# Sums over keys placed directly in front of the mix of values, and a mix that leaves PSUM undivided

## The chip, the cores and the metric

The kernel runs on one core of a Trainium2 chip. The metric is the device time of one launch in microseconds (us). The kernel before took 2891.65 us, the median of three runs (2891.22 to 2893.65).

The engines are called as the profile calls them: PE is TensorE (matmuls and transposes; PEld are its weight loads), DVE is VectorE, ACT is ScalarE, POOL is GpSimd, SP is SyncE, which here only issues DMAs.

## The reference, cut to what matters

Two graph layers run over 64 graphs ("batches") of 256 nodes with 512 features in f32. The first is attention with 8 heads of 64 under one adjacency mask, the second a graph attention with one score per node pair. Each adds its input and normalises:

```python
q, k, v = (x @ Wq + bq), (x @ Wk + bk), (x @ Wv + bv)          # split into 8 heads of 64
scores = einsum('bqhd,bkhd->bhqk', q, k) / sqrt(64) + (1 - adj) * -1e9
attn = softmax(scores, axis=-1)                                 # over the keys
x = layernorm(x + einsum('bhqk,bkhd->bqhd', attn, v) @ Wo + bo)
h = x @ W
e = leaky_relu(s1[:, :, None] + s2[:, None, :]) * adj           # s1, s2: h times the halves of a
x = layernorm(x + elu(softmax(e, axis=2) @ h + beta * h))
```

The change touches the line with `attn` and the one below it: the division of the softmax by its sums over the keys, and the mix of values.

## The kernel before

Every batch goes through twelve named stages. Their names are those of `ROUND` (L23):

- **x**: `tr_x` transposes the input tile (L496) into xT.
- **q, k, v**: projections by `project` (L382 and L386). Each is written as seven products of quarter matrices, with the sums of quarters on POOL (`token_sums`, L360: xS, oS, yS) and the results combined by ACT copies and DVE additions (L517, L520, L526). The products lie in three PSUM tiles, ps_chain, ps_cross and ps_pair.
- **scores**: `ps_sc` (L574), keys on partitions, two heads at a time on the two halves of the array's rows (64*128). DVE adds the mask (L581), ACT takes the exponential (L583), POOL adds the two key tiles of a head into `both` (L585).
- **sums**: `ps_den` (L597), the sums over the keys, by matmuls against columns of ones, on four groups of 32 columns (128*32). DVE takes the reciprocal (L601), ACT notes the range of both (L604). A DMA writes the 8 rows to DRAM (L607) and two more bring them back spread over the partitions as `inv_all` (L611), in the code `everywhere`.
- **mix**: `ps_pv` (L551), values times exponentials, two heads at a time on the two halves of the columns (128*64). DVE multiplies the PSUM result by `everywhere` into oT (L617).
- **o**: the output projection from oT and its POOL differences oS, added to x on DVE (L700), then the layer norm (L456 to L466).
- **logits**: the two scores of a node by DVE (L715), their transposes `tr_s` (L725), then the mask, the maximum and the exponential on DVE, POOL and ACT.
- **attention**: `tr_a` transposes the probabilities (L753), ACT copies them to attT (L757).
- **spread**: `ps_y` (L768), probabilities times x; **u**: the projection by W; then elu, the norm and the store of the result.

The order is not left to the hardware. Every piece of work is registered with `plan.op` (engine, an assumed duration, what it reads and writes, and for PE a `mode`: the shape in which the array is used). PE's order is fixed by a pair per piece, the number of its round and the place of its stage in `ROUND`. The pair comes from `turn`, which adds to the batch's number n a delay in rounds: with "sums": 0 and "mix": 1, the sums of batch n are in round n and its mix in round n + 1. The other engines get due times from PE's order, and `place` lists everything greedily against slots of buffers (8 PSUM banks, 9 SBUF tiles of the tag "full", 24 of "half", 5 of x). The last 70 pieces of PE are ordered freely (`OPEN`). A round of the kernel before reads on PE:

    tr_a, mix, scores, tr_x, ps_y, o, u, sums, v, tr_s, q, k

Each of the stages works on a batch of its own: while the scores are those of batch n, the mix and o are those of n - 1, and tr_a, spread and u those of n - 2. In order that the mix can be multiplied by `everywhere` on its way out of PSUM, the reciprocals of a batch have to be back from DRAM when its mix ends; the piece "mix" on PE therefore lists `everywhere` among its reads.

[...]

There is a second form of the attention for inputs whose sums leave a safe range (`attention_by_queries`); it doesn't run with these inputs.

Of the kernel before, what the change touches and what calls it, by code (L numbers as in the profile page):

```python
# [19 lines left out]
ALPHA = 0.2  # L20
NEG = -1000000000.0

ROUND = ("mix", "scores", "x", "spread", "o", "u", "sums", "v", "logits", "q", "k", "attention")  # L23
SAFE = 1e15


# [196 lines left out]
def gnn_two_layers(ctx: ExitStack, tc: tile.TileContext, x, adj, Wq, bq, Wk, bk, Wv, bv, Wo, bo, W, a, beta, out):  # L223
    nc = tc.nc
# [23 lines left out]
    plan = Plan(slots)  # L248
    stay = []
    A = slice(None)  # L250

    def sb(tag, shape, name):
        return Buf(sb_pool, tag, [P] + shape, name)

    def ps(shape, name):
        return Buf(ps_pool, "ps", [P] + shape, name)
# [11 lines left out]
    def blk(t):  # L268
        return slice(t * P, (t + 1) * P)
# [142 lines left out]
    def residual_bias():  # L412
        bo_sb = for_now(bo, 0, "bo")
        acc = ps([D], "ps_b")

        def pe():
            for c in range(C):
                nc.tensor.matmul(acc[A], bv_sb[:, c:c + 1].to_broadcast([P, P]), wo_sb[:, c, :], start=c == 0,
                                 stop=c == C - 1)

        plan.op("PE", 3440, pe, [wo_sb], [acc], claims=[res_sb])
        plan.op("DVE", 690, lambda: nc.vector.tensor_add(res_sb[A], acc[A], bo_sb[A]), [acc, bo_sb], [res_sb])  # L422
        return weight_sums(wo_sb, "so_sb", "POOL", [res_sb])
# [46 lines left out]
    def batch(b, at, general=False):  # L470

        X = sb("x", [NT, D], f"x_{b}")
        n = b or 0

        def turn(what):

            later = {"x": -1, "q": -1, "k": -1, "scores": 0, "v": 0, "sums": 0, "mix": 1, "o": 1, "logits": 1,
                     "attention": 1, "spread": 2, "u": 2}[what]
            plan.turn = (n + later, ROUND.index(what if b != 0 or what != "sums" else "logits"))

        plan.op("SP", 2800, lambda: nc.sync.dma_start(X[A], x[at].rearrange("o (t p) d -> p (o t) d", p=P)), [],
                [(X, (t, i)) for t in range(NT) for i in range(2)], first=b == 0)
# [6 lines left out]
        V = sb("full", [NT, D], f"v_{b}")  # L489
# [14 lines left out]
        if b == 0:  # L504
            plan.turn = (0, ROUND.index("spread"))
            left["o"] = residual_bias()
# [27 lines left out]
        def val():  # L534
            turn("v")
            project(lv, right, False, [V], *gather(lambda q: (lambda: V[:, q[1], half(q[0])], (V, q))))


        oT = sb("full", [C, N], f"oT_{b}")

        def mixed(pT, g, onto, reads=()):

            turn("mix")
            acc = ps([2, N], "ps_pv")

            def pe():
                for i in range(2):
                    for k in range(NT):
                        for s in range(2):
                            h = 4 * g + 2 * i + s  # L550
                            nc.tensor.matmul(acc[s * HD:(s + 1) * HD, i, :], V[:, k, h * HD:(h + 1) * HD],  # L551
                                             pT[h][:, k, :], start=k == 0, stop=k == NT - 1)

            plan.op("PE", 1740, pe, [(V, (g, 0)), (V, (g, 1))] + pT[4 * g:4 * g + 4] + list(reads), [acc],
                    mode="columns", claims=[oT])
            plan.op("DVE", 690, lambda: onto(acc), [acc] + list(reads), [(oT, g)])

        def attention_by_keys():

            pT = [sb("half", [NT, N], "pT") for h in range(H)]  # L560
            both = [sb("half", [2, N], "both") for c in range(C)]
            inv, everywhere = sb("half", [N], "inv"), sb("full", [C, N], "inv_all")
            rows = Buf(dram_pool, "rows", [H, N], "rows")

            def scores(g):
                turn("scores")
                acc = [ps([NT, N], "ps_sc") for _ in range(4)]

                def pe():
                    for i in range(0, 4, 2):  # L570
                        for k in range(NT):
                            for s in range(2):
                                h, r = 4 * g + i + s, s * HD
                                nc.tensor.matmul(acc[i + s][:, k, :], kT[r:r + HD, h // 2, blk(k)],  # L574
                                                 qT[r:r + HD, h // 2, :], start=True, stop=True)

                plan.op("PE", 1740, pe, [(m, (g, j)) for m in (qT, kT) for j in range(NT)], acc, mode="rows",
                        claims=pT[4 * g:4 * g + 4] + both[2 * g:2 * g + 2])
                for i in range(4):
                    h = 4 * g + i  # L580
                    plan.op("DVE", 690, lambda h=h, i=i: nc.vector.tensor_add(pT[h][A], acc[i][A], maskT_sb[A]),  # L581
                            [acc[i], maskT_sb], [pT[h]])
                    plan.op("ACT", 620, lambda h=h: nc.scalar.activation(  # L583
                        pT[h][A], pT[h][A], AF.Exp, scale=1.0 / HD ** 0.5), [pT[h]], [pT[h]])
                    plan.op("POOL", 725, lambda h=h: nc.gpsimd.tensor_tensor(  # L585
                        both[h // 2][:, h % 2, :], pT[h][:, 0, :], pT[h][:, 1, :], ALU.add),
                        [pT[h]], [(both[h // 2], h % 2)])

            def denominators():
                turn("sums")  # L590

                acc = ps([N], "ps_den")

                def pe():
                    for s in range(2):
                        for c in range(C):
                            nc.tensor.matmul(acc[32 * c:32 * c + 32, :], ones[:, 16 - 16 * s:48 - 16 * s],  # L597
                                             both[c][:, s, :], start=s == 0, stop=s == 1)

                plan.op("PE", 1000, pe, both, [acc], mode="sums", claims=[inv])  # L600
                plan.op("DVE", 1750, lambda: nc.vector.reciprocal(inv[A], acc[A]), [acc], [inv])  # L601
                for i, m in enumerate((acc, inv)):
                    junk = sb("half", [N], "junk")
                    plan.op("ACT", 600, lambda i=i, m=m, junk=junk: nc.scalar.activation(  # L604
                        junk[A], m[A], AF.Identity, accum_out=range_sb[:, i, b:b + 1]), [m],
                        [junk, (range_sb, (i, b))])
                plan.op("SP", 60, lambda: nc.sync.dma_start(rows[A], inv[0:P:P // H, :]), [inv], [rows])  # L607
                for s in range(2):
                    def spread(s=s):
                        r = rows[A]  # L610
                        nc.sync.dma_start(everywhere[s * HD:(s + 1) * HD], bass.AP(  # L611
                            tensor=r.tensor, offset=r.offset + s * N, ap=[[0, HD], [2 * N, C], [1, N]]))

                    plan.op("SP", 1500, spread, [rows], [(everywhere, s)])

            def mix(g):
                mixed(pT, g, lambda acc: nc.vector.tensor_mul(  # L617
                    oT[:, 2 * g:2 * g + 2, :], acc[A], everywhere[:, 2 * g:2 * g + 2, :]), [everywhere])

            scores(0)  # L620
            scores(1)
            val()
            denominators()
            mix(0)
            mix(1)

        def attention_by_queries():
# [32 lines left out]
            pT = [sb("half", [NT, N], "pT") for h in range(H)]  # L660

            def flip(h):
                turn("mix")
                tr = ps([NT, N], "tr_p")

                def pe():
                    for k in range(NT):
                        for t in range(NT):
                            nc.tensor.transpose(tr[:, k, blk(t)], pr[t][h // 4][:, h % 4, blk(k)], ident)

                plan.op("PE", 430, pe, [pr[t][h // 4] for t in range(NT)], [tr], claims=[pT[h]])
                if h % 2:
                    plan.op("ACT", 580, lambda: nc.scalar.copy(pT[h][A], tr[A]), [tr], [pT[h]])
                else:
                    plan.op("DVE", 690, lambda: nc.vector.tensor_copy(pT[h][A], tr[A]), [tr], [pT[h]])
# [5 lines left out]
            for g in range(2):  # L681
                for h in range(4 * g, 4 * g + 4):
                    flip(h)
                mixed(pT, g, lambda acc, g=g: nc.vector.tensor_copy(oT[:, 2 * g:2 * g + 2, :], acc[A]))

        turn("q")
        qk(lq, bq_sb, qT)
# [10 lines left out]
        def onto(q, acc):  # L698
            i, j = q
            plan.op("DVE", 420, lambda: nc.vector.tensor_add(  # L700
                X[:, j, half(i)], X[:, j, half(i)], acc[1]()), [acc[0], (X, (j, i))], [(X, (j, i))])
# [10 lines left out]
        for t in range(NT):  # L712
            for i in range(2):
# [4 lines left out]
                    mode="two")  # L718
# [62 lines left out]
        u = sb("full", [NT, D], f"u_{b}")  # L781
# [43 lines left out]
    with tc.If(again != 0):  # L825
# [3 lines left out]
        with tc.For_i(0, B, 1) as i:  # L829
            for tile_ in stay:  # L830
                tile_.parts = {}
            plan = Plan({**slots, "half": slots["half"] - 1})
# [33 lines left out]
```

## Time and profile before

| | busy us | share of the span |
|---|---|---|
| PE (matmuls) | 2852.6 | 99% |
| PEld (weight loads, beside the matmuls) | 2477.5 | 86% |
| DVE | 1895.8 | 66% |
| POOL | 1361.9 | 47% |
| ACT | 1293.3 | 45% |
| DMA, mean of 16 engines (queue q1) | | 11.3% |

The span is 2892.0 us, at a mean granted clock of 0.995. An engine's share says how full it is, not what it costs: what an engine does beside a full PE is free as long as PE doesn't wait for it. The costliest groups on the path of the change are these (count, mean of one):

| line | what | count | mean ns |
|---|---|---|---|
| L551 | PE mix ps_pv, 128*64 | 2048 | 382 |
| L574 | PE scores ps_sc, 64*128 | 2048 | 382 |
| L597 | PE sums ps_den, 128*32 | 1024 | 385 |
| L617 | DVE oT <- ps_pv, inv_all, 128x512 | 128 | 692 |
| L601 | DVE reciprocal of ps_den, 128x256 | 64 | 1752 |
| L360 | POOL oS <- oT, 128x256 | 128 | 732 |

A matmul's length in the profile (382 ns) includes its latency and overlaps with the next one's; the distance from start to start is what a matmul costs in a stream. The DMA list has inv_all with 128 issues of 256 KB, 3.6 us from issue to landing, and the load of x with 64 issues of 512 KB and 3.7 us.

### The profile page before, as it was taken

How to read it: one execution, taken by the hardware profiler on the slowest of the kernel's cores; microseconds unless marked ns; L12 is line 12 of the kernel's file. 1: busy time of each engine (PE TensorE's matmuls, PEld its weight loads, DVE VectorE, ACT ScalarE, POOL GpSimd, SP SyncE). 2: the span in 40 equal slices, each digit the busy share in tenths (PEclk: the TensorE clock that was granted, in tenths of full speed). 3: DMA queues.
4: the chain of work that ended last, by engine and by line, in shares of the span. 5: the costliest groups of instructions: out<-in, count | busy, mean ns of one | idle time of the engine just before them, and what ended most of it. 6: DMA issues, size and time to landing. Idle time of an engine off the chain costs nothing.

```text
span 2892.0 us, 51909 instructions
## 1 busy us (share of the span) xinstructions
PE 2852.6 (99%) x19605; PEld 2477.5 (86%) x19605; DVE 1895.8 (66%) x4322; ACT 1293.3 (45%) x3201; POOL 1361.9 (47%) x2010
## 2 busy tenths in 40 slices
PE   8999999999999999999999999999999999999996
PEld 7888888888888888888888888888888888888884
DVE  5666666666666666666666666666666666666666
ACT  3444444444444444444444444444444444444442
POOL 6454453553544544535535445445355354454543
PEclk9999999999999999999999999999999999999998
DMA  3001011011011010111110110111101101111000
GB/s 132 24 30 45 30 38 45 30 38 44 25 44 38 30 45 30 38 45 30 37 45 23 45 37 31 45 30 37 45 30 38 45 23 45 35 33 45 30 23 31
DMA packets 75407, 110.89 MB, mean 38 GB/s; under 512 B 5904, under 2 KB 39440, under 8 KB 75152
## 3 DMA queue, kind: packets, MB, share of 16 engines
q1 hardware_dynamic: 75024, 107.50, 11.3%
q8 instruction: 158, 2.59, 0.4%
q14 instruction: 97, 0.79, 0.1%
q0 software_dynamic: 128, 0.01, 0.0%
HBM read 73.41 MB, written 34.08 MB: 37 GB/s over the span
## 4 chain that ended last, share of the span: by engine, by line
PE 97%; DVE 1%; POOL 1%; issue 0%; DMA 0%; ACT 0%; POOLq 0%; DVEq 0%
PE ps_chain L386 17%; PE ps_chain L382 12%; PE ps_pair L386 11%; PE ps_cross L386 11%; PE ps_cross L382 8%; PE ps_pair L382 8%; PE ps_sc L574 8%; PE ps_pv L551 8%; PE ps_y L768 8%; PE tr_x L496 2%; PE ps_den L597 2%; PE tr_a L753 1%; PE tr_s L725 0%; DVE junk L715 0%; DMA beta_sb<-in_L_gnn_beta_dram 0%
## 5 line engine op out<-in xcount | busy, mean ns | idle before, releaser
L360 POOL TENSOR_TENSOR oS<-oT 128x256 f32<-128x256 f32 x128 | 93.7, 732 | 725.1 <-DVE oT L617 720.0
L583 ACT ACTIVATE pT<-pT 128x512 f32<-128x512 f32 x512 | 297.7, 627 | 303.2 <-DVE pT L581 303.2
L735 POOL TENSOR_TENSOR e<-e,adj_sb 128x512 f32<-128x512 f32 x64 | 81.6, 1275 | 662.4 <-DVE e L733 656.4
L585 POOL TENSOR_TENSOR both<-pT 128x256 f32<-128x256 f32 x512 | 360.9, 734 | 35.8 <-ACT pT L583 35.8
L581 DVE TENSOR_TENSOR pT<-ps_sc,maskT_sb 128x512 f32<-128x512 f32 x512 | 317.4, 682 | 22.8 <-PE ps_sc L574 22.7
L517 ACT COPY u<-ps_chain 128x256 f32<-128x256 f32 x128 | 47.6, 372 | 442.6 <-PE ps_chain L386 442.6
L574 PE MATMUL ps_sc<-qT,kT 64*128 64x256 f32 x2048 | 238.4, 382 | 0.0
L768 PE MATMUL ps_y<-attT,x 128*128 128x256 f32 x1024 | 236.0, 384 | 1.4 <-ACT attT L757 1.4
L551 PE MATMUL ps_pv<-pT,v 128*64 128x256 f32 x2048 | 235.1, 382 | 0.0
L574 PEld LDWEIGHTS ps_sc<-qT,kT 64*128 64x128 f32 x2048 | 192.8, 187 | 43.8 <-issue 24.0
L768 PEld LDWEIGHTS ps_y<-attT,x 128*128 128x128 f32 x1024 | 192.0, 193 | 26.7 <-ACT attT L757 2.2
L551 PEld LDWEIGHTS ps_pv<-pT,v 128*64 128x64 f32 x2048 | 141.4, 137 | 75.5 <-issue 10.3
L466 ACT ACTIVATE x<-x,nmr,rs 128x512 f32<-128x512 f32 x256 | 194.5, 809 | 17.4 <-DVE nmr L464 17.4
L617 DVE TENSOR_TENSOR oT<-ps_pv,inv_all 128x512 f32<-128x512 f32 x128 | 88.5, 692 | 162.2 <-PE ps_pv L551 162.2
L700 DVE TENSOR_TENSOR x<-x,ps_chain 128x256 f32<-128x256 f32 x256 | 102.1, 420 | 138.0 <-PE ps_chain L386 137.2
L715 DVE SCALAR_TENSOR_TENSOR junk<-x,wa_sb 128x512 f32<-128x512 f32 x256 | 165.3, 701 | 0.9 <-ACT x L466 0.9
L501 POOL TENSOR_TENSOR x<-x,res_sb 128x512 f32<-128x512 f32 x128 | 164.4, 1285 | 3.1 <-DVE res_sb L422 3.1
L456 DVE BATCH_NORM_STATS2 bn<-x 128x6 f32<-128x512 f32 x256 | 164.1, 683 | 2.2
L520 ACT ACTIVATE qT<-ps_chain,bq_sb 128x128 f32<-128x128 f32 x256 | 80.3, 365 | 187.9 <-PE ps_chain L382 187.9
L461 POOL TENSOR_TENSOR rs<-rs,neg_half 128x1 f32<-128x1 f32 x256 | 144.2, 563 | 21.3
L382 PE MATMUL ps_chain<-xS,sq_sb 128*128 128x128 f32 x1024 | 135.9, 276 | 0.0
L382 PE MATMUL ps_chain<-xS,sk_sb 128*128 128x128 f32 x1024 | 135.4, 275 | 0.0
(174 smaller groups left out, 6799.0 us busy)
## 6 DMA issues: line engine op xcount, KB each, us to landing
x<-in_x_dram SPq DMA_DIRECT2D x64, 512.0 KB, 3.7
inv_all<-rows SPq DMA_DIRECT2D x128, 256.0 KB, 3.6
out_dram<-x SPq DMA_DIRECT2D x128, 256.0 KB, 2.0
wq_sb<-in_L_gnn_Wq_dram SPq DMA_DIRECT2D x1, 1024.0 KB
wk_sb<-in_L_gnn_Wk_dram SPq DMA_DIRECT2D x1, 1024.0 KB
wo_sb<-in_L_gnn_Wo_dram SPq DMA_DIRECT2D x1, 1024.0 KB
wv_sb<-in_L_gnn_Wv_dram SPq DMA_DIRECT2D x1, 1024.0 KB
w_sb<-in_L_gnn_W_dram SPq DMA_DIRECT2D x1, 1024.0 KB, 14.4
```

Source lines behind the costliest of these rows:

```text
L382: nc.tensor.matmul(dst[:, f, :], l[:, c, blk(f)], r[:, c, :], start=start and f == 0 and c == 0, stop=c == 1, skip_group_check=True)
L386: nc.tensor.matmul(dst, r[:, c, :], l[:, c, :], start=start and c == 0, stop=c == 1, skip_group_check=True)
L456: plan.op("DVE", 690, lambda: nc.vector.bn_stats(bn[A], X[:, t, :]), [(X, (t, 0)), (X, (t, 1))], [bn])
L466: plan.op("ACT", 810, lambda: nc.scalar.activation(X[:, t, :], X[:, t, :], AF.Identity, bias=nm[A], scale=rs[A]), [nm, rs], [(X, (t, 0)), ...
L501: plan.op("POOL", 1270, lambda: nc.gpsimd.tensor_tensor(X[:, t, :], X[:, t, :], res_sb[A], ALU.add), [res_sb], tokens(t))
L551: nc.tensor.matmul(acc[s * HD:(s + 1) * HD, i, :], V[:, k, h * HD:(h + 1) * HD], pT[h][:, k, :], start=k == 0, stop=k == NT - 1)
L574: nc.tensor.matmul(acc[i + s][:, k, :], kT[r:r + HD, h // 2, blk(k)], qT[r:r + HD, h // 2, :], start=True, stop=True)
L581: plan.op("DVE", 690, lambda h=h, i=i: nc.vector.tensor_add(pT[h][A], acc[i][A], maskT_sb[A]), [acc[i], maskT_sb], [pT[h]])
L583: plan.op("ACT", 620, lambda h=h: nc.scalar.activation(pT[h][A], pT[h][A], AF.Exp, scale=1.0 / HD ** 0.5), [pT[h]], [pT[h]])
L585: plan.op("POOL", 725, lambda h=h: nc.gpsimd.tensor_tensor(both[h // 2][:, h % 2, :], pT[h][:, 0, :], pT[h][:, 1, :], ALU.add), [pT[h]], [ ...
L715: plan.op("DVE", 780, lambda t=t, i=i, junk=junk: nc.vector.scalar_tensor_tensor(junk[A], X[:, t, :], 1.0, wa_sb[:, i, :], op0=ALU.mult, o ...
L768: nc.tensor.matmul(acc[:, i, :], X[:, j, c * P:(c + 1) * P], attT[:, j, :], start=j == 0, stop=j == NT - 1)
```

## The change

It has three parts.

1. `ROUND` gets another order, and with "sums": 1 the sums of a batch come in the same round as its mix, directly ahead of it. The attention of the second layer gets a delay of 2 in place of 1, which with its new place behind the scores leaves it in about the same spot of the stream. v comes behind it, ahead of x; o and u stay neighbours; the logits stand between q and k. The special place of the first batch's sums goes.
2. The piece "mix" no longer reads `everywhere`. Its result leaves PSUM undivided, by an ACT copy into oT.
3. DVE multiplies oT in SBUF by `everywhere`, in place, when that has landed (mode "two"). POOL's differences oS, which read oT, come behind that.

What it is for: the three stages that don't use the array as a whole, sums, mix and scores, stand side by side, so that the array's shape is changed fewer times in a round; and the way of the reciprocals through DRAM no longer stands between the sums and the mix. A round of the changed kernel reads on PE:

    sums, mix, scores, tr_a, v, tr_x, ps_y, o, u, q, tr_s, k

```diff
-ROUND = ("mix", "scores", "x", "spread", "o", "u", "sums", "v", "logits", "q", "k", "attention")
+ROUND = ("sums", "mix", "scores", "attention", "v", "x", "spread", "o", "u", "q", "logits", "k")
...
-            later = {"x": -1, "q": -1, "k": -1, "scores": 0, "v": 0, "sums": 0, "mix": 1, "o": 1, "logits": 1,
-                     "attention": 1, "spread": 2, "u": 2}[what]
-            plan.turn = (n + later, ROUND.index(what if b != 0 or what != "sums" else "logits"))
+            later = {"x": -1, "q": -1, "k": -1, "scores": 0, "v": 0, "sums": 1, "mix": 1, "o": 1, "logits": 1,
+                     "attention": 2, "spread": 2, "u": 2}[what]
+            plan.turn = (n + later, ROUND.index(what))
...
-            plan.op("PE", 1740, pe, [(V, (g, 0)), (V, (g, 1))] + pT[4 * g:4 * g + 4] + list(reads), [acc],
+            plan.op("PE", 1740, pe, [(V, (g, 0)), (V, (g, 1))] + pT[4 * g:4 * g + 4], [acc],
                     mode="columns", claims=[oT])
-            plan.op("DVE", 690, lambda: onto(acc), [acc] + list(reads), [(oT, g)])
+            onto(acc)
...
             def mix(g):
-                mixed(pT, g, lambda acc: nc.vector.tensor_mul(
-                    oT[:, 2 * g:2 * g + 2, :], acc[A], everywhere[:, 2 * g:2 * g + 2, :]), [everywhere])
+                part = slice(2 * g, 2 * g + 2)
+
+                def onto(acc):
+                    plan.op("ACT", 590, lambda: nc.scalar.copy(oT[:, part, :], acc[A]), [acc], [(oT, g)])
+                    plan.op("DVE", 690, lambda: nc.vector.tensor_mul(
+                        oT[:, part, :], oT[:, part, :], everywhere[:, part, :]), [everywhere], [(oT, g)], mode="two")
+
+                mixed(pT, g, onto)
```

The function `attention_by_queries` gets the same division of work, with the DVE copy that it had.

## The prediction

> **What bounds the kernel now.** I read the head of the page first: one engine is full.
>
> ```profile
> span 2892.0 us, 51909 instructions
> PE 2852.6 (99%) x19605; PEld 2477.5 (86%) x19605; DVE 1895.8 (66%) x4322; ACT 1293.3 (45%) x3201; POOL 1361.9 (47%) x2010
> ...
> PE 97%; DVE 1%; POOL 1%; issue 0%; DMA 0%; ACT 0%; POOLq 0%; DVEq 0%
> ```
>
> Second line: TensorE (PE) is busy for 99% of the span, the next engine for 66%. Third line, the chain that ended last: 97% of it is PE following PE. So almost no wait can be removed from PE; a gain has to come out of PE's own stream. A busy PE can still lose time between instructions, so I went to the timeline of PE in a round in mid-run (columns: start, length, what; the length is modelled, so I use differences of starts).
>
> ```profile
> 1514.46 0.60 PE L753 MATMUL tr_a<-ident,e 128*128 128x128 f32 x4
> 1514.99 3.67 PE L551 MATMUL ps_pv<-pT,v 128*64 128x256 f32 x32
> 1518.59 3.72 PE L574 MATMUL ps_sc<-qT,kT 64*128 64x256 f32 x32
> 1522.25 1.09 PE L496 MATMUL tr_x<-ident,x 128*128 128x128 f32 x8
> 1523.17 3.62 PE L768 MATMUL ps_y<-attT,x 128*128 128x256 f32 x16
> 1526.63 1.03 PE L386 MATMUL ps_chain<-wo_sb,oT 128*128 128x256 f32 x4
> ...
> 1537.85 1.03 PE L386 MATMUL ps_chain<-sw_sb,yS 128*128 128x256 f32 x4
> 1538.81 1.07 PE L597 MATMUL ps_den<-both,ones 128*32 128x256 f32 x16
> 1539.81 1.13 PE L386 MATMUL ps_chain<-wv_sb,xT 128*128 128x256 f32 x4
> 1540.78 1.03 PE L386 MATMUL ps_cross<-wv_sb,xT 128*128 128x256 f32 x4
> ```
>
> No line carries a wait, and the round repeats every 44.23 us (sums start at 1538.81 and, 28 rounds later, at 2777.16). What is to be seen is the excess. A 128x256 matmul costs 0.216 us (16 of ps_y in 3.46), a full-array 128x128 transpose 0.109. Wherever the shape in front of the arrow (128*128, 128*64, 64*128, 128*32) changes, the stage before the change or the first product after it is longer than that:
> - tr_a takes 0.530 for 4 transposes (0.436): 0.094 over, just ahead of the mix;
> - mix ps_pv takes 3.604, 16 pairs at 0.216 are 3.453: 0.151 over;
> - scores ps_sc 3.655 against 3.453: 0.202;
> - tr_x behind the scores 0.928 against 0.874: 0.054;
> - the last product of u 0.96 against 0.864: 0.096, just ahead of the sums;
> - sums ps_den 1.001 for 4 groups of four at 0.216 (0.864): 0.137;
> - the first product of v behind them 0.97 against 0.864: 0.105.
>
> That is 0.84 us a round in all. A product of v whose neighbours have its own shape shows no excess.
>
> **What the Trainium skill says.** "TensorEngine Tiling (Array Packing)", section Tiling Modes, states that a change of tiling mode, not of tile, drains the engine. The seven terms above agree: each sits at a change, and nothing else is late. It lists 128x64 and 128x32 as different configurations, so the pair sums/mix would still pay; no place in this trace has these two side by side. "SBUF — State Buffer", section Who interferes with whom, states that a VectorE (DVE) instruction with two SBUF inputs contends with a GpSimd (POOL) instruction that reads SBUF. The new multiply is of that kind; how long POOL would be held is bounded below. "TensorE: Matmul & The Clock Gate", section Part 1, states that after about 3.4 us of idling the array runs at half clock. The start of this run agrees: after two idle stretches of 2.32 and 1.96 us
>
> ```profile
> 81.42 0.32 PE L725 MATMUL tr_s<-ident,s 128*128 128x128 f32 x1 [2.32 <-DVE junk L715]
> 83.70 0.48 PE L725 MATMUL tr_s<-ident,s 128*128 128x128 f32 x1 [1.96 <-DVE junk L715]
> 83.97 1.92 PE L382 MATMUL ps_chain<-xT,wq_sb 128*128 128x128 f32 x8
> ```
>
> a product of q takes 1.71 from start to start in place of 0.893 (the last line).
>
> **The change, part by part.** *The order of the round.* In the program as built, the steady PE stream runs: q, tr_s, k, sums, mix, scores, tr_a, v, tr_x, ps_y, o, u. No matmul is added or dropped. Changes of shape: before five (into sums, out of sums, into mix, mix to scores, out of scores), after four. Term by term: the 0.096 in front of the sums now stands at the end of k; sums, mix and scores keep 0.137 + 0.151 + 0.202; the 0.054 behind the scores falls on tr_a in place of tr_x. Two terms have no successor: the first product of v (0.105) and the end of tr_a (0.094). Gain 0.199 us a round; about 61 rounds are steady, so 61 x 0.199 = 12.1 us.
>
> The untested joint is sums to mix. Lower bound of its cost: nothing, as if both were one shape. Of the sums' 0.137, at most about 0.11 is the end (u, tr_a show 0.095 there), of the mix's 0.151 some 0.05 the start; the gain would then be 0.36 a round, 22 us. Upper bound: as costly as sums to v, whose start took 0.105 in place of 0.05; gain 0.144, 8.8 us. I take the middle, the drain of any change and the start of the mix as it is now.
>
> *The mix leaves PSUM undivided.* Per round two ACT copies of 128x512 are added. The same copy of tr_a to attT (L757) takes 586 ns: 1.17 us on an engine that is 45% busy; around the mix ACT stood idle for 4.75 us up to the exponentials (L583), which hides both. They release the two banks of ps_pv at least as early as DVE did at 692 ns. DVE's two multiplies stay, at 0.69 (both sources in SBUF: L791 has 695 ns, bound 0.68 to 0.70), and move behind the eight mask additions (L581). Cost on PE: nothing, if what follows holds.
>
> *The wait that is added.* The mix no longer waits for `everywhere`; o does, by the multiply and POOL's four differences. Counting from the start of the sums: 1.0 sums, 0.3 to the reciprocal, 1.75 reciprocal (L601), 1.77 from the issue of rows to that of inv_all, 0.63 second issue, 3.6 landing, 2 x 0.69 multiply, four differences at 0.81 spacing 3.2: 13.6 us. The next load of x (512 KB, 3.7 us to landing) stands between rows and inv_all on the SP queue: 17.3 at the most. The start of o comes at 1.0 + 3.6 + 3.66 + 0.53 + 6.04 + 0.93 + 3.46 = 19.2. Slack 1.9 us, and o begins with a quarter that needs no difference. Queued behind the multiply on DVE are three additions into v; they free banks for tr_x and ps_y. DVE is done with the mask additions about 1.2 + 8 x 0.68 = 6.6 us after scores began (at 4.6), so at 11.2. inv_all has landed at 9.1 without the load of x ahead, at 12.8 with all of it; in that worst case the multiplies end at 14.2 and v's cross addition, due at 13.1, is 1 us late, which the other free banks should absorb. POOL, 47% busy, may be held for 1.4 us and has the sums of x due only at 31.
>
> *Logits.* From the end of o to tr_s there were v, sums and u (13.3 us), now u and q (12.3); DVE's last junk ended 9.1 us after o. Slack 3. tr_a now follows k, sums, mix and scores (14.5 us after tr_s), before q and k (12.5). Both cost nothing in steady rounds.
>
> *Start and end.* At the start the first tr_s has only q(2) ahead of it (6.3 us), where sums and v (7.2) stood: its wait of 4.3 us may grow by 1, but v(0) needs no res_sb work in front. I take 0, give or take 3. At the end PE idled 5.9 us between the logits of batch 62 and u of 62, and ran at low clock for some 3 us more; after the change o of batch 63 lies between these logits and tr_a, which fills about 5 us, while the split of mix and scores there adds two or three changes of shape. I take a gain of 2.
>
> Sum: 2891.65 - 12.1 - 2 = 2877.5 us.
>
> **The rivals.**
> - *Sums and mix need no drain between them.* For it: both use all 128 rows, only the columns differ. Against: the tiling page, and tr_a to mix, also 128 rows on both sides, pays. 2891.65 - 22 - 2 = 2868, halfway 2872.
> - *The joint costs as much as sums to v.* 2891.65 - 8.8 - 2 = 2881.
> - *A new wait replaces the drain.* o waits for the multiply because inv_all lands behind the load of x, or a bank of v comes free late. For it: the slack is only 1.9 us, and POOL and DVE can each be one instruction (0.7 us) into something else. Against: before, POOL waited on the old multiply for 720 us in all, so it is not short of time. With 0.3 us a round, 2877.5 + 61 x 0.3 = 2896; with half of it, 2886.
>
> **How the numbers follow.** Forecast 0.62 at 2877.5; no drain 0.14 at 2872 to 2868; dear joint 0.08 at 2881; new wait 0.16, of which 0.06 end near 2886 to 2891 and 0.10 slower. Faster (below 2885.9) is 0.62 + 0.14 + 0.08 = 0.84, same 0.06, slower 0.10. The range takes in the free joint at one end and, on the other, the dear joint with 3 us lost at the start and half of a new wait: 2868 to 2888.
>
> **What would show it.** In the timeline after: the first product of v at 0.86, tr_a 0.49 behind the scores, k's last product 0.99, sums still 1.00, period 44.03. A period of 43.9 or less tells of the free joint; a wait entered at o (DVE oT or POOL oS), at v or ps_y (banks), or at tr_s tells of the new wait. It is wrong if the period does not shrink.

## The result, and the profile after

The changed kernel took 2877.65 us (median of four runs, 2876.74 to 2877.90) against 2892.19 us for the kernel before (four runs, 2891.22 to 2893.65). The ratio is 0.9949, with a 95% interval of 0.9932 to 0.9966: 14.5 us less.

The head of the page and its chain of waits, in the kernel after:

```profile
span 2875.9 us, 51742 instructions
...
PE 2839.2 (99%) x19605; PEld 2484.7 (86%) x19605; DVE 1937.1 (67%) x4322; ACT 1366.9 (48%) x3329; POOL 1403.3 (49%) x2010
...
PE 98%; DVE 1%; POOL 0%; DMA 0%; issue 0%; ACT 0%; POOLq 0%; DVEq 0%; ACTq 0%
```

PE issues the same 19605 matmuls and is as full as before; its busy time fell by 13.4 us. ACT has 128 instructions more and 73.6 us more to do, DVE 41.3 us and POOL 41.4 us more, and none of them is near its limit. So the gain lies inside PE's stream. A round of it, from the timeline of PE in mid-run (start, length, what):

```profile
1499.54 1.06 PE L382 MATMUL ps_chain<-xS,sk_sb 128*128 128x128 f32 x8
1500.52 1.07 PE L597 MATMUL ps_den<-both,ones 128*32 128x256 f32 x16
1501.52 3.67 PE L551 MATMUL ps_pv<-pT,v 128*64 128x256 f32 x32
1505.13 3.72 PE L574 MATMUL ps_sc<-qT,kT 64*128 64x256 f32 x32
1508.78 0.66 PE L760 MATMUL tr_a<-ident,e 128*128 128x128 f32 x4
1509.28 1.03 PE L386 MATMUL ps_chain<-wv_sb,xT 128*128 128x256 f32 x4
1510.14 1.03 PE L386 MATMUL ps_cross<-wv_sb,xT 128*128 128x256 f32 x4
```

Read the differences of starts: the last product of k takes 0.98, the sums 1.00, the mix 3.61 (3.604 on average), the scores 3.65, tr_a 0.50, the first product of v 0.86. Averaged over fifty rounds, each against the same stage of before (q, tr_s, ps_y and o are the same to 0.002):

| stage, from its start to the next one's | before, us | after, us |
|---|---|---|
| u (before, the sums follow it) | 6.137 | 6.043 |
| k (after, the sums follow it) | 6.253 | 6.347 |
| sums | 1.001 | 1.001 |
| mix | 3.604 | 3.604 |
| scores | 3.655 | 3.655 |
| tr_a | 0.530 | 0.493 |
| v | 6.148 | 6.046 |
| tr_x | 0.928 | 0.873 |
| a whole round | 44.227 | 44.030 |

A round is 0.196 us shorter. From the first round in which both streams have the same work behind them and stand in front of mix, scores and tr_a (before, tr_a comes first of the three, at 99.21 us; after, the mix, at 92.56) to the last such one (2752.80 and 2734.37) lie 60 rounds, 11.8 us. What is ahead of this stretch became 6.65 us shorter, what is behind it 2.3 us longer: 6.65 + 11.8 - 2.3 = 16.1, the difference of the two profiled spans. The profiled run of before took 2893.83 us, 1.6 above its median, so some 1.6 us of the 16.1 are spread from run to run.

### The profile page after: what moved, and what is told of

Same layout as the page of the kernel before. It is cut to its first block, busy times and chain, and to the rows that moved or that the text cites. A ratio compares the mean times of both kernels' runs of the same rounds, so it can differ in the third digit from the quotient of the medians.

```text
span 2875.9 us, 51742 instructions
## 1 busy us (share of the span) xinstructions
PE 2839.2 (99%) x19605; PEld 2484.7 (86%) x19605; DVE 1937.1 (67%) x4322; ACT 1366.9 (48%) x3329; POOL 1403.3 (49%) x2010
## 4 chain that ended last, share of the span: by engine, by line
PE 98%; DVE 1%; POOL 0%; DMA 0%; issue 0%; ACT 0%; POOLq 0%; DVEq 0%; ACTq 0%
PE ps_chain L386 17%; PE ps_chain L382 12%; PE ps_cross L386 11%; PE ps_pair L386 11%; PE ps_sc L574 8%; PE ps_cross L382 8%; PE ps_pv L551 8%; PE ps_pair L382 8%; PE ps_y L775 8%; PE ps_den L597 2%; PE tr_x L496 2%; PE tr_a L760 1%; PE tr_s L732 0%; DMA beta_sb<-in_L_gnn_beta_dram 0%; DVE junk L722 0%
## 5 line engine op out<-in xcount | busy, mean ns | idle before, releaser
L585 POOL TENSOR_TENSOR both<-pT 128x256 f32<-128x256 f32 x512 | 389.4, 782 | 718.4 <-ACT pT L583 710.1
L460 POOL TENSOR_SCALAR rs<-mv 128x1 f32<-128x1 f32 x256 | 57.8, 226 | 544.2 <-DVE mv L457 541.9
L707 DVE TENSOR_TENSOR x<-x,ps_chain 128x256 f32<-128x256 f32 x256 | 101.9, 419 | 173.1 <-PE ps_chain L386 173.0
L456 DVE BATCH_NORM_STATS2 bn<-x 128x6 f32<-128x512 f32 x256 | 164.4, 683 | 2.3
L501 POOL TENSOR_TENSOR x<-x,res_sb 128x512 f32<-128x512 f32 x128 | 160.3, 1275 | 1.9 <-DVE res_sb L422 1.9
L520 ACT ACTIVATE kT<-ps_chain,bk_sb 128x128 f32<-128x128 f32 x256 | 80.1, 363 | 162.6 <-PE ps_chain L382 162.6
L601 DVE RECIPROCAL inv<-ps_den 128x256 f32<-128x256 f32 x64 | 112.5, 1757 | 39.6 <-PE ps_den L597 39.2
## 6 DMA issues: line engine op xcount, KB each, us to landing
wv_sb<-in_L_gnn_Wv_dram SPq DMA_DIRECT2D x1, 1024.0 KB, 12.8
w_sb<-in_L_gnn_W_dram SPq DMA_DIRECT2D x1, 1024.0 KB, 12.8
```

The source lines that it names most:

```text
L456: plan.op("DVE", 690, lambda: nc.vector.bn_stats(bn[A], X[:, t, :]), [(X, (t, 0)), (X, (t, 1))], [bn])
L501: plan.op("POOL", 1270, lambda: nc.gpsimd.tensor_tensor(X[:, t, :], X[:, t, :], res_sb[A], ALU.add), [res_sb], tokens(t))
L585: plan.op("POOL", 725, lambda h=h: nc.gpsimd.tensor_tensor(both[h // 2][:, h % 2, :], pT[h][:, 0, :], pT[h][:, 1, :], ALU.add), [pT[h]], [ ...
```

## The experiments

The theory: the gain in a round is one change of the array's shape fewer, four in place of five (sums to v and tr_a to mix go, sums to mix comes), and nothing else in the round pays; the change of shape between sums and mix is still paid. Rivals: that joint is free; or the undivided mix brings the gain itself; or the gain lies at the start of the run.

### The new way out of PSUM alone: mix_undivided_only

The changed kernel with the order of before.

```diff
-ROUND = ("sums", "mix", "scores", "attention", "v", "x", "spread", "o", "u", "q", "logits", "k")
+ROUND = ("mix", "scores", "x", "spread", "o", "u", "sums", "v", "logits", "q", "k", "attention")
...
-            later = {... "sums": 1, ... "attention": 2, ...}[what]
-            plan.turn = (n + later, ROUND.index(what))
+            later = {... "sums": 0, ... "attention": 1, ...}[what]
+            plan.turn = (n + later, ROUND.index(what if b != 0 or what != "sums" else "logits"))
```

> The order of a round as before, with the mix leaving PSUM by an ACT copy and multiplied in SBUF. Theory of shape changes: the array changes shape as often as before, so the period of a round stays 44.23 us, the start and the end stay as they were to 1 us, and the time is 2892 us, within 2 us of the kernel before. Rival, the undivided mix itself brings the gain (PSUM released earlier, no wait of the mix for the reciprocals): a period near 44.03 us and about 2878 us. If the multiply in SBUF holds up POOL so that PE waits, it is slower than 2894 us.

Measured: 2893.88 us (13 runs, 2892.84 to 2895.14), ratio 1.0006 [0.9997, 1.0014]. Every stage has its length of before (u 6.137, v 6.148, tr_a 0.530), the round 44.23 us. Two places of it, the end of tr_a (0.53 to the mix) and the first product of v (0.97):

```profile
1515.01 0.60 PE L760 MATMUL tr_a<-ident,e 128*128 128x128 f32 x4
1515.54 3.67 PE L551 MATMUL ps_pv<-pT,v 128*64 128x256 f32 x32
```

```profile
1496.14 1.13 PE L386 MATMUL ps_chain<-wv_sb,xT 128*128 128x256 f32 x4
1497.11 1.02 PE L386 MATMUL ps_cross<-wv_sb,xT 128*128 128x256 f32 x4
```

So the copies and the multiply in SBUF cost and bring nothing by themselves; the whole gain needs the order.

### Sums and mix pulled apart: tr_x_between_sums_and_mix

```diff
-ROUND = ("sums", "mix", "scores", "attention", "v", "x", "spread", "o", "u", "q", "logits", "k")
+ROUND = ("sums", "x", "mix", "scores", "attention", "v", "spread", "o", "u", "q", "logits", "k")
```

> The changed kernel with one stage of full array shape, tr_x, moved between the sums and the mix; everything else of the change is there. Theory of shape changes: one more change to the full shape and one more back. From the terms of the kernel before: the start of transposes behind another shape 0.054 us and the end of a transposing stage ahead of the mix 0.094 us, together 0.148 us a round, so a period of 44.18 us and about 2877.7 + 61 x 0.148 = 2886.7 us. Rival, the gain comes from the undivided mix or from the start and the end: period 44.03 and 2878 us. If the earlier tr_x makes PE wait for a buffer, a wait shows at tr_x or v and it is slower than 2890 us.

Measured: 2885.93 us (13 runs, 2884.61 to 2888.86), ratio 0.9981 [0.9972, 0.9989], the round 44.178 us. The timeline of PE in this kernel:

```profile
1505.48 1.07 PE L597 MATMUL ps_den<-both,ones 128*32 128x256 f32 x16
1506.48 1.09 PE L496 MATMUL tr_x<-ident,x 128*128 128x128 f32 x8
1507.50 3.67 PE L551 MATMUL ps_pv<-pT,v 128*64 128x256 f32 x32
```

tr_x takes 1.02 us between two other shapes; among neighbours of its own shape it took 0.873 in the kernel after. The sums and the mix keep their 1.00 and 3.60. One more change of shape in a round costs 0.148 us, the same 60 times: 8.9 us, and the two kernels' medians differ by 8.3. This is the direct test of the order: what pays is that the narrow stages stand side by side.

### Sums in the mix's own shape: sums_in_shape_of_mix

The columns of ones are widened to 64, so that the sums use the array as 128*64, at the price of eight groups in place of four.

```diff
-    ones = const.tile([P, 48], F32, name="ones")
+    ones = const.tile([P, 112], F32, name="ones")
...
-                    for s in range(2):
-                        for c in range(C):
-                            nc.tensor.matmul(acc[32 * c:32 * c + 32, :], ones[:, 16 - 16 * s:48 - 16 * s],
-                                             both[c][:, s, :], start=s == 0, stop=s == 1)
+                    for i in range(4):
+                        for j in range(2):
+                            nc.tensor.matmul(acc[64 * j:64 * j + 64, :], ones[:, 48 - 16 * i:112 - 16 * i],
+                                             both[2 * j + i // 2][:, i % 2, :], start=i == 0, stop=i == 3)
...
```

> The changed kernel with the sums computed on two groups of 64 columns, the shape of the mix, in place of four groups of 32: eight pairs at 0.216 us where four groups stood, 0.864 us more a round. It prices the joint between sums and mix, which the prediction left open. If two column shapes that differ drain the array like any change (0.11 end of the sums, 0.05 start of the mix, 0.03 more at the start of the sums for 64 columns): without the joint the mix starts at once, so only 0.864 - 0.16 + 0.03 = 0.73 us more a round, a period of 44.76 and 2877.7 + 61 x 0.73 = 2922 us. If the joint costs nothing for its shape, the end of the sums staying for another reason: 44.03 + 0.864 + 0.03 = 44.92 us and 2932 us.

Measured: 2921.74 us (4 runs, 2921.11 to 2922.23), ratio 1.0101 [1.0084, 1.0118]; the round 44.76 us. Its PE timeline:

```profile
1525.29 1.95 PE L597 MATMUL ps_den<-both,ones 128*64 128x256 f32 x16
1527.07 3.62 PE L551 MATMUL ps_pv<-pT,v 128*64 128x256 f32 x32
```

The sums take 1.777 us: eight groups at 0.216 (1.726) and 0.051 over. The mix takes 3.553, 0.100 over, where it was 0.151: its late start, 0.050, is gone, and the end of the sums shows no excess either. This can be read at the joint itself. Here are the last matmuls of the sums, the first of the mix and, on PEld, the first weight loads of the mix, in the kernel after:

```profile
1501.19 0.40 PE L597 MATMUL ps_den<-both,ones 128*32 128x256 f32 x4
1501.52 0.44 PE L551 MATMUL ps_pv<-pT,v 128*64 128x256 f32 x2
1501.52 0.20 PEld L551 LDWEIGHTS ps_pv<-pT,v 128*64 128x64 f32 x4 [0.41 <-issue]
```

and in this run, where both stages have one shape:

```profile
1526.86 0.39 PE L597 MATMUL ps_den<-both,ones 128*64 128x256 f32 x2
1527.07 0.39 PE L551 MATMUL ps_pv<-pT,v 128*64 128x256 f32 x2
1526.86 0.36 PEld L551 LDWEIGHTS ps_pv<-pT,v 128*64 128x64 f32 x4
```

From the last group of the sums to the mix pass 0.33 us across the change and 0.21 without it. So the joint costs 0.113 us at the end of the sums and 0.050 at the start of the mix, 0.163 in all. (The difference of the two stages as wholes is smaller, 0.288 over against 0.151, because the sums also start 0.027 us later in 128*64 than in 128*32.) The expectation for a joint that drains, 0.73 us more a round, is met with 0.725. The joint isn't free, and the four groups more (0.863) cost far more than it.

The loads show what else happens there: across the change the first weight load of the mix starts together with its matmul, without it 0.21 us ahead, together with the last matmuls of the sums.

### The first batch's logits behind its q: first_logits_behind_q

The kernel before, with the logits of batch 0 alone put behind q.

```diff
             plan.turn = (n + later, ROUND.index(what if b != 0 or what != "sums" else "logits"))
+            if b == 0 and what == "logits":
+                plan.turn = (n + later, ROUND.index("q") + 0.5)
```

> The kernel before, with one edit of the order that touches the first batch alone: its logits come behind q of the third batch instead of ahead of it, as they do in the changed kernel. In the kernel before PE idles 4.28 us there and then runs four products at about half clock (2.7 us lost). If the part of the gain at the start (6.6 us by the two traces) comes from this place: the waits of 2.32 and 1.96 us and the slow products go, a wait of 1 to 2 us for the probabilities comes at the first tr_a, rounds in mid-run stay at 44.23 us, and the time is 2892 - 5.5 = 2886.5 us. If the start gained for another reason (the place of v or of the first load of weights): 2891 to 2892 us.

Measured: 2887.09 us (18 runs, 2885.70 to 2888.96), ratio 0.9983 [0.9976, 0.9990], steady rounds 44.23 us as before. The wait at the first tr_a that was expected did not come. PE waited 1.23 us inside q for a bank that DVE had still to read, and tr_s then ran without a wait. The kernel before, run beside it, had a median of 2892.59 us. So the start of the kernel before can be mended by two lines, for 5.5 us, without touching the steady round.

### The new order with the division left in PSUM: new_order_divided_mix

The kernel before with `ROUND` and `turn` of the change; the piece "mix" on PE still lists `everywhere`, and DVE still multiplies out of PSUM.

```diff
-ROUND = ("mix", "scores", "x", "spread", "o", "u", "sums", "v", "logits", "q", "k", "attention")
+ROUND = ("sums", "mix", "scores", "attention", "v", "x", "spread", "o", "u", "q", "logits", "k")
...
+            later = {... "sums": 1, ... "attention": 2, ...}[what]
+            plan.turn = (n + later, ROUND.index(what))
```

> The new order of a round with the mix as in the kernel before: PE lists the reciprocals among the reads of the mix, DVE multiplies on the way out of PSUM. Theory: the order can't pay alone, since the reciprocals need a way of about 0.3 + 1.75 + 1.77 + 0.63 + 3.6 to 4.7 us = 8 to 9 us from the end of the sums to the last landing, and now the mix stands right behind the sums. PE idles 8 to 9 us in each of some 61 rounds, and runs about 3 us more after each at a low clock: a period of 53 to 56 us, 3430 to 3600 us. Rival, that the order alone brings the gain: 2878 us.

Measured: 3316.33 us (one run). The expectation missed both the size and the place. PE did not stop ahead of the mix; these are two stretches of its timeline and, below, DVE's:

```profile
1530.62 2.86 PE L574 MATMUL ps_sc<-qT,kT 64*128 64x256 f32 x24
1538.04 2.67 PE L574 MATMUL ps_sc<-qT,kT 64*128 64x256 f32 x8 [4.56 <-DVE oT L617]
```

```profile
1537.30 1.29 DVE L617 TENSOR_TENSOR oT<-ps_pv,inv_all 128x512 f32<-128x512 f32 x2 [7.13 <-DMA inv_all<-rows]
1538.51 4.86 DVE L581 TENSOR_TENSOR pT<-ps_sc,maskT_sb 128x512 f32<-128x512 f32 x8
```

The mix's matmuls don't read `everywhere`, so nothing in the instruction waits for it. Its name among the reads works on the planner alone. In the order that came out of it DVE has the two multiplies ahead of the eight mask additions, and there stands 7.13 us for the DMA. The scores, whose PSUM banks those additions empty, stop after 24 of 32 matmuls. Over the rounds the scores stage takes 9.15 us on average in place of 3.655 (10.03 in the one shown), and v behind it 7.30 in place of 6.05: in the round shown the granted clock is at 0.50 for 6.8 us from 1536.81 on.

### The same, without `everywhere` in PE's reads: new_order_multiply_from_psum

```diff
-            plan.op("PE", 1740, pe, [(V, (g, 0)), (V, (g, 1))] + pT[4 * g:4 * g + 4] + list(reads), [acc],
+            plan.op("PE", 1740, pe, [(V, (g, 0)), (V, (g, 1))] + pT[4 * g:4 * g + 4], [acc],
```

> The new order; PE no longer lists the reciprocals among the reads of the mix, but DVE multiplies out of PSUM as before, so the two banks of the mix are held until inv_all has landed. It splits the second part of the change in two: PE without the wait (kept), ACT's copy that frees the banks early (left out). If only PE's wait matters: scores needs eight banks with two held, DVE frees one each 0.68 us from 1.7 us after scores began, which is in time for heads 6 and 7 at 2.7 us, and the time stays at 2876 to 2880 us with a period of 44.03 us. If the early release of the banks is what makes the order possible: waits of PE at scores, tr_a or v, 0.5 us a round or more, over 2905 us.

Measured: 2877.16 us (4 runs, 2876.61 to 2877.70), ratio 0.9948 [0.9931, 0.9965], the stages of the kernel after. The multiplies now stand behind the mask additions on DVE and hold two PSUM banks until then, at no cost to PE that can be measured. So ACT's copy, the second part of the change, isn't needed for the gain; what is needed beside the order is that the planner no longer ties the mix to the reciprocals.

### How much slack the new wait has: one_more_hop, two_more_hops

Between the write of the reciprocals to DRAM and their reading, one or two more copies from DRAM to DRAM are put in (and the slots for `rows` go from 4 to 12).

```diff
+                far = rows
+                for hop in range(2):          # range(1) in one_more_hop
+                    near, far = far, Buf(dram_pool, "rows", [H, N], "rows")
+                    plan.op("SP", 60, lambda near=near, far=far: nc.sync.dma_start(far[A], near[A]), [near], [far])
...
-                        r = rows[A]
+                        r = far[A]
```

> The changed kernel with one more copy of the reciprocals from DRAM to DRAM ahead of inv_all, which makes the way 1.8 to 2.2 us longer. It tests the slack of the wait that the change adds at o. In the trace of the changed kernel the fourth difference oS ends 17.3 us after the sums began and o starts at 19.2: 1.9 us of slack at the first product, more at the later ones. If so: at most 0.3 us of wait a round, 2877 to 2896 us. If o is already just in time: a wait at o of about 2 us a round, 3000 us.

> The changed kernel with two more copies of the reciprocals through DRAM, 3.5 to 4.4 us longer. One more hop cost nothing. Here the planner puts DVE's multiplies behind the copy of the spread's result, about 17.6 to 18.3 us after the sums began, so oT is undivided until 19.7 to 20 us and the differences end at 23, while o could start at 19.2. If the added wait has some 2 us of slack: it is used up, PE waits at o for 0.5 to 2 us a round, 2908 to 3000 us, the wait shown at the first products of o. If the wait has no bite at all: 2877 us.

Measured with one hop: 2876.93 us (one run), all stages as in the kernel after. The hop was longer than expected: inv_all is issued 3.7 us later, where 1.8 to 2.2 had been put. POOL's differences end 3.6 us later against the start of the sums (20.9 us, without the hop 17.3), and PE waits for none of them. With two: 3069.3 us (one run), above the range expected. The timeline of PE in that kernel, where o begins:

```profile
1528.44 1.13 PE L386 MATMUL ps_chain<-wo_sb,oT 128*128 128x256 f32 x4
1531.41 1.62 PE L386 MATMUL ps_cross<-wo_sb,oT 128*128 128x256 f32 x4 [1.85 <-POOL oT L360]
1532.83 1.91 PE L386 MATMUL ps_pair<-wo_sb,oT 128*128 128x256 f32 x4
1534.53 1.43 PE L386 MATMUL ps_chain<-so_sb,oS 128*128 128x256 f32 x4
```

The wait that the third rival of the prediction spoke of is here: o for oT, by way of the differences on POOL, 60 times, 1.83 us on average. In this round o takes 9.95 us in place of 6.04, 3.91 more, of which the wait is 1.85. Most of the rest is the clock. The view of a stretch (start and end; length; busy time of PE, PEld, DVE, ACT and POOL with instruction counts; granted clock; share of DMA; GB/s):

```profile
1531.92:1535.33 3.41, 3.41 (x9) 2.70 (x9) 0.84 (x2) 0.00 (x0) 3.17 (x6) 0.50 0.00 0
```

Half a microsecond after the wait the clock is at 0.50 for 3.41 us, and the three products from 1531.41 on take 1.42, 1.70 and 1.27 us from start to start in place of 0.864. But not every round looks like this. Three rounds later the same wait costs no clock:

```profile
1675.60 1.13 PE L386 MATMUL ps_cross<-wo_sb,oT 128*128 128x256 f32 x4 [1.85 <-POOL oT L360]
1676.57 1.03 PE L386 MATMUL ps_pair<-wo_sb,oT 128*128 128x256 f32 x4
```

```profile
1675.60:1681.00 5.40, 5.40 (x25) 4.78 (x26) 2.11 (x5) 0.00 (x0) 4.99 (x7) 1.00 0.00 0
```

There o takes 8.26 us. Of 59 such rounds 34 lose the clock and take 9.95, 25 don't; the mean is 3.19 us more than without the wait.

### The free end: open_50, before_open_50

The changed kernel, and the kernel before, with fewer pieces ordered freely at the end.

```diff
-    OPEN = 70
+    OPEN = 50
```

> The changed kernel with the last 50 pieces of PE ordered freely in place of 70. The change lost about 2.3 us at the end, by the two traces: the last o ends late, and the chain from it (norm, logits, probabilities, spread, u) sets the end. With 50 the last o stands whole ahead of the transposes of the batch before, and scores and mix aren't split. If the order of the last pieces sets the end: 3 to 6 us faster than the changed kernel, 2872 to 2875 us, with the same 44.03 us a round. If the end is set by the latency of the last batch alone whatever stands around it: 2877 to 2878 us.

> The kernel before with the last 50 pieces of PE ordered freely in place of 70, for the comparison with the changed kernel at 50. Rounds in mid-run stay at 44.23 us. If what the 6 us at 50 came from is the order of the last pieces in general, this one gains too: 2885 to 2890 us. If 50 only mends what the changed order of a round spoiled at the end (2.3 us): 2891 to 2894 us.

Measured: the changed kernel with 50 took 2871.41 us (5 runs, 2867.70 to 2872.22), ratio 0.9926 [0.9913, 0.9940], faster than both kernels and 0.6 below the range expected; its rounds are the same 44.03 us. The kernel before with 50 took 2894.68 us (12 runs, 2893.32 to 2895.81), ratio 1.0009 [1.0001, 1.0018]. So 50 isn't better in general; it suits the end of this order. PE at the end of the changed kernel with 50:

```profile
2833.06 0.27 PE L732 MATMUL tr_s<-ident,s 128*128 128x128 f32 x1
2835.00 0.32 PE L732 MATMUL tr_s<-ident,s 128*128 128x128 f32 x1 [1.67 <-DVE junk L722]
...
2843.39 0.85 PE L760 MATMUL tr_a<-ident,e 128*128 128x128 f32 x4 [1.20 <-DVE e L751]
```

Six products of u lie between tr_s and the last tr_a, which waits 1.20 us; in the changed kernel itself one product lies there and the wait is 7.42 (shown below). In exchange PE waits 4.05 us in the last o, for DVE (L707).

## Why the prediction was right, and where its terms were off

The time forecast was 2877.5 us and the measured 2877.65. That closeness is partly luck: the step that carries it was right, and two others were wrong in opposite directions.

**The order of the round** was right in mechanism, place and size: 0.199 us a round forecast, 0.196 measured, the two missing terms at v and tr_a. The sums, mix and scores each kept their excess, u's went to k (6.347 - 6.253 = 0.094), and tr_x's 0.055 to tr_a. Undoing the order (mix_undivided_only) takes the gain away whole, and opening one joint (tr_x_between_sums_and_mix) takes 0.148 a round of it.

**The joint of sums and mix.** The middle was taken between free and dear, about 0.11 at the end of the sums and 0.05 at the start of the mix; measured were 0.113 and 0.050. The rival of a free joint (2868 to 2872) fell by sums_in_shape_of_mix. What the Trainium skill says in "TensorEngine Tiling (Array Packing)", section Tiling Modes, that 128x64 and 128x32 are different configurations and that a change of configuration drains the engine, agrees here, with 0.163 us for this pair.

**The mix leaves PSUM undivided.** That it costs PE nothing was right. The multiply was mis-sized: 0.68 to 0.70 us were allowed, and it took this (lengths: shortest, median, longest in ns):

```profile
L621 DVE TENSOR_TENSOR oT<-oT,inv_all x128: 674/984/1215, 66.0 to 2811.4; 128x512 f32<-128x512 f32 x128
```

In the round shown above the multiplies meet POOL's additions. First DVE, then POOL, in the kernel after:

```profile
1512.48 2.11 DVE L621 TENSOR_TENSOR oT<-oT,inv_all 128x512 f32<-128x512 f32 x2
```

```profile
1507.78 2.11 POOL L585 TENSOR_TENSOR both<-pT 128x256 f32<-128x256 f32 x3 [9.92 <-ACT pT L583]
1511.32 2.73 POOL L585 TENSOR_TENSOR both<-pT 128x256 f32<-128x256 f32 x3 [1.43 <-ACT pT L583]
...
1517.09 0.72 POOL L360 TENSOR_TENSOR oS<-oT,oS 128x256 f32<-128x256 f32 x1
```

Two multiplies take 2.11 us where 1.38 were forecast, and three additions beside them 2.73 where three without take 2.11. In new_order_multiply_from_psum, where one source is in PSUM, the same multiply took 671 to 693 ns, and the 512 additions (L585) 731 ns on average, where they took 734 in the kernel before and 782 in the kernel after. In one_more_hop the multiplies come later and have both sources in SBUF all the same:

```profile
L625 DVE TENSOR_TENSOR oT<-oT,inv_all x128: 678/688/1764, 66.5 to 2811.0; 128x512 f32<-128x512 f32 x128
```

There 67 of them take 0.68 to 0.69, and 59, which fall on POOL's L501 (128x512), 1.76. So it is the company that stretches them. The Trainium skill says in "SBUF — State Buffer", section Who interferes with whom, that a DVE instruction with two SBUF inputs contends with a POOL instruction that reads SBUF; the traces agree, with 0.98 and 1.21 us in the kernel after in place of 0.69. The planner's mode "two", which is there to keep such a DVE piece and POOL's pieces apart in time, did not do so here.

**The wait that is added** was worked out well enough to bear this. Counted from the start of the sums (1500.52) the multiplies end at 14.1 us (worst case forecast 14.2), the last difference at 17.3 (forecast 17.3), o starts at 19.1 (forecast 19.2). The longer multiplies fit into the same time because they began at 12.0, where the worst case had 12.8. The landing of inv_all went from 3.6 to 4.7 us in the page's median, with the load of x in front of it on its queue, as foreseen. The slack, 1.8 us measured, was on the safe side, since the products that need the differences come later in o: one more hop took 3.6 us and was still hidden. The rival of a new wait describes a true danger, reached at two hops, and was priced too low: at 0.3 us a round, where a wait of 1.85 cost 3.19 on average.

The account of what the wait *replaces* was loose. The mix on PE never waited for `everywhere` in the program; only DVE's multiply did. Its place among PE's reads set the order of DVE's queue, as new_order_divided_mix and new_order_multiply_from_psum show: the two kernels differ in nothing else.

**Logits**: right, no wait at tr_s in steady rounds (4 waits in the whole run, 3.5 us).

**The start** failed: 0 forecast, give or take 3, and it gained 6.65 us. In the kernel after:

```profile
83.92 0.29 PE L732 MATMUL tr_s<-ident,s 128*128 128x128 f32 x1 [0.17 <-DVE junk L722]
85.05 0.32 PE L732 MATMUL tr_s<-ident,s 128*128 128x128 f32 x1 [0.84 <-DVE junk L722]
```

The waits fell from 4.28 to 1.01 us, and with them the products at half clock behind them (four took 6.30 us in place of 3.57, 2.7 us more). The wrong step was to count what PE has ahead of tr_s (6.3 against 7.2 us) and to take DVE's way there as fixed. This is DVE in the kernel *before*, computing the logits of the first batch, and then POOL beside it:

```profile
78.06 1.62 DVE L715 SCALAR_TENSOR_TENSOR junk<-x,wa_sb 128x512 f32<-128x512 f32 x1
...
79.62 1.73 DVE L715 SCALAR_TENSOR_TENSOR junk<-x,wa_sb 128x512 f32<-128x512 f32 x1
...
81.28 1.74 DVE L715 SCALAR_TENSOR_TENSOR junk<-x,wa_sb 128x512 f32<-128x512 f32 x1
```

```profile
79.10 3.37 POOL L501 TENSOR_TENSOR x<-x,res_sb 128x512 f32<-128x512 f32 x2
```

Three of the four dot products take 1.62 to 1.74 us where the fourth takes 0.68, beside POOL's quarter sums of a weight (L346) and its preparation of x (L501); that is 3.05 us more, and the reciprocal of the sums (1.72), which stood between o and tr_s in the old order, comes on top. In the kernel after POOL had done L501 at 79.2, the sums lie elsewhere, and the same four take 0.69 each. first_logits_behind_q shows that the stall was worth 5.5 us. It also shows that the overlap with POOL doesn't make a stall by itself: there the dot products are as slow (one of them below), but q stands ahead of tr_s, and PE doesn't wait at tr_s.

```profile
80.23 1.75 DVE L717 SCALAR_TENSOR_TENSOR junk<-x,wa_sb 128x512 f32<-128x512 f32 x1
```

How much of the 6.65 us the overlap is worth was not tried by itself.

**The end** failed too: a gain of 2 forecast, 2.3 lost. PE and DVE at the end of the kernel after:

```profile
2839.84 0.38 PE L732 MATMUL tr_s<-ident,s 128*128 128x128 f32 x2
2840.26 1.13 PE L386 MATMUL ps_pair<-w_sb,yS 128*128 128x256 f32 x4
2848.82 1.21 PE L760 MATMUL tr_a<-ident,e 128*128 128x128 f32 x4 [7.42 <-DVE e L751]
```

```profile
2840.38 0.86 DVE L738 TENSOR_SCALAR z<-tr_s,s 128x256 f32<-128x256 f32 x2
...
2842.82 1.57 DVE L800 SCALAR_TENSOR_TENSOR x<-m,x 128x512 f32<-128x512 f32 x1
...
2846.08 0.68 DVE L744 TENSOR_REDUCE nm<-e 128x2 f32<-128x512 f32 x1
```

The prediction took the 5.92 us of before for a wait of the last batch but one, which o of the last would fill. Behind it there are only one ps_y and one u: it belongs to the last batch, whose o is done by then, in both kernels. So no o could fill it; what can is u of the batch before, as in open_50. By the traces it grew to 7.42 us because the free ordering now put the norm of the batch before (L798, L800, L456) into DVE's queue between z and the maximum nm: 5.70 us from one to the other, where it was 3.41 before and is 3.04 in open_50.

Together: 4.3 us from start and end where 2 were assumed, or about 2.8 if the 1.6 us by which the profiled run of before lies above its median are taken off. With 11.8 in the rounds that makes the 14.5 us, beside 14.1 forecast. Each of these two terms was off by more than 4 us, the start by more than the 3 it was given.

## What to carry to other kernels

When the array is full, list the excess of each stage over its matmuls times their slot and put stages of narrow shape side by side; the changes of shape in the loop that go, less those that come, each at its price (here 0.12 to 0.22 us), give the gain before anything is built. A read that is listed only for a planner can move the queue of a third engine: look at what it reorders there, not only at who waits for it. At the two ends of the run count the queue of the engine that feeds the next stage, with what runs beside it, and tune the free end anew after a change of order; here that was worth another 6 us.

## What the runs showed of the hardware that was not expected

- A change of shape shows on both sides of it. Behind the last matmul of the old shape it costs 0.09 us more than a matmul of its kind, whatever the two shapes are (0.100 and 0.113 for a group of two or four matmuls side by side, which start a little apart). At the start of the new shape it costs 0.02 for the sums in 128*32, 0.05 for 128*64, 0.055 for the transposes, 0.10 for the scores and for the first product of v. So u to sums costs 0.12, sums to mix 0.16, sums to v 0.22. A detour by the whole array between sums and mix adds 0.148, about one step more.
- At every change of shape the first weight load of the new shape starts within 0.003 us of its matmul; at every other border of two stages it starts 0.11 to 0.21 us ahead, with the last matmul of the old stage. This holds for all steady rounds of before, after, tr_x_between_sums_and_mix and sums_in_shape_of_mix. Whether the late load makes the excess or only comes with it, no run separates.
- A wait of 1.85 us was enough to halve the granted clock for 3.41 us, in 34 of 59 rounds of two_more_hops. The Trainium skill names about 3.4 us of idling for this in "TensorE: Matmul & The Clock Gate", section Part 1; the wait measured here is shorter, and it decides. Neither of the two waits at the start of the kernel before, 2.32 and 1.96 us, which the prediction took to agree with the page, was that long either. In these rounds the half-clock stretches start on one grid with a step of 3.41 us. Where a point of the grid fell well inside the wait (1.6 to 2.9 us after the start of o), in 18 rounds, the clock stayed full in all 18; in the other 41 it fell in 34. So the same wait cost 2.2 or 3.9 us, by where it lay.
- DVE instructions of 128x512 with two SBUF sources stretched from 0.68 us to 0.98 and 1.21 beside POOL's 128x256 additions, and to 1.74 to 1.76 beside its 128x512 one. The POOL side paid as well: 1.69 us for each of the two L501 in the kernel before's start, where the median of this line is 1.28.
